# A threshold search by two bits a round on VectorE and ScalarE, and the small first loads moved to GpSimd

## The chip, the cores and the metric

The kernel runs on one core of one Trainium2 chip. The metric is the device time of one execution in microseconds (us). The engines are TensorE (PE in the profile's rows; PEld is its weight load), VectorE (DVE), ScalarE (ACT), GpSimd (POOL) and SyncE (SP). A letter q behind an engine's name means the queue that issues its transfers.

## What is computed

A GRU runs over 256 steps for 16 rows of width 512. Its 4096 states are the tokens of an "expert choice" layer: each of 16 experts takes its 256 best tokens by router probability, and what the one shared expert matrix makes of a token is weighted by the sum of the probabilities of the experts that took it.

```python
def cell(h, x):
    gi = x @ W_ih + b_ih
    gh = h @ W_hh + b_hh
    r = sigmoid(i_r + h_r);  z = sigmoid(i_z + h_z)
    n = tanh(i_n + r * h_n)
    return (1.0 - z) * n + z * h

S = softmax(xf @ router_w + router_b)        # 4096 tokens, 16 experts
G, idx = top_k(S.T, 256)
out = xf[idx] @ expert_w + expert_b
y = zeros(4096, 512).at[idx].add(G[..., None] * out)
return x + y
```

The top 256 of an expert are found as a threshold: the largest float32 that at least 256 of its 4096 probabilities reach. Probabilities are positive, so the order of the floats is the order of their bit patterns read as whole numbers.

## The kernel before, in words

**Head.** Constants (an identity, and masks that say which partitions belong to one expert) are made by GpSimd and VectorE in lines 86 to 106, in a pool of scratch memory that is given back afterwards and in which later tiles, the weights `wih` among them, come to lie. Then SyncE and ScalarE issue the weight loads in an order written out by hand (lines 272 to 285): for each of three gates of `W_ih` two loads of 512 KB, one on each queue; x of the first eight steps (`xa0`, eight loads of 32 KB, line 236) behind the first pair; then the three gates of `W_hh`; then x of the next eight steps (`xa1`, in the same buffer as `xa0`), the expert and router weights and two biases. GpSimd issues four bias loads (line 266) and four loads of the initial state (line 268). `turn_x` (line 252) transposes `xa`; the x parts of the first two pairs of steps (line 396) follow, and the recurrence.

**Recurrence.** For each step TensorE adds the products with `whh` (line 409), ScalarE takes sigmoid and tanh (lines 465, 486, 487), VectorE does the rest (lines 482 to 505). In what room is left TensorE computes the expert's product for even groups of eight steps. Fifteen groups are done so; 17 are *late groups*: the odd ones and group 30.

**Late groups.** A late group's product takes eight parts (`late_part`, line 136), each of four matmuls that the trace shows as eight records. `expert_for(n)` puts n parts into TensorE's queue at the place where it is called, so that they fill TensorE beside other work. At a group's fifth part the bank of the next group but one is filled with the expert's bias by ScalarE (`pe<-eb`, line 156; for the first three also cleared by TensorE, line 112); after the eighth ScalarE evicts the sum (`ht<-pe`, line 173). Five banks go round. Once the gate is known, a group isn't evicted any more: line 670 reads its bank.

**Search.** After the softmax the probabilities lie transposed in `sT`, 512 columns on each of 128 partitions, eight partitions an expert. The search sets one bit a round, from bit 29 down, in 30 rounds: VectorE compares all 512 columns with the candidate and sums along the partition (line 599), a TensorE matmul with `same_h` adds the eight partitions of an expert (line 604), `expert_for(2 or 3)` follows, and two small VectorE operations make the next candidate (lines 607 and 610). The order on TensorE, ScalarE and VectorE is the program's from line 570 on (`manual_schedule`).

**Routing and output.** Lines 621 to 662 settle ties and make `gate`, 32 columns of weights. Line 670 then makes the 32 output groups one after another, the fifteen early groups first and the late ones in order, and SyncE stores each (line 673, 256 KB). Where a late group isn't done, its remaining parts stand in TensorE's queue there.

Of the kernel before, what the change touches and what calls it, by code (L numbers as in the profile page):

```python
# [18 lines left out]
def kernel(  # L19
# [61 lines left out]
    same_h = const.tile([P, P], F16, name="same_h")  # L81
    before_f = const.tile([P, P], F32, name="before_f")
# [4 lines left out]
    make_identity(nc, ident)  # L87
    nc.gpsimd.memset(ones_b, 1.0)
    with tc.tile_pool(name="masks", bufs=1) as mk:
        shift = GH.bit_length() - 1  # L90
        at = mk.tile([P, 3], I32, name="at")
# [3 lines left out]
        at_f = mk.tile([P, 3], F32, name="at_f")  # L95
        nc.vector.tensor_copy(at_f, at)
        to_i = mk.tile([P, 2, E, GH], I32, name="to_i")
        nc.gpsimd.iota(to_i[:, 0, :, :], pattern=[[1, E], [0, GH]], base=0, channel_multiplier=0)
        nc.gpsimd.iota(to_i[:, 1, :, :], pattern=[[0, E], [1, GH]], base=0, channel_multiplier=0)
        to = mk.tile([P, 2, P], F32, name="to")  # L100
        nc.vector.tensor_copy(to, to_i.rearrange("p o e h -> p o (e h)"))
        nc.vector.tensor_scalar(same_f, to[:, 0, :], at_f[:, 1:2], None, ALU.is_equal)
        nc.vector.tensor_copy(same_h, same_f)
        nc.vector.tensor_scalar(before_f, to[:, 1, :], at_f[:, 2:3], None, ALU.is_gt)
# [79 lines left out]
    with (  # L184
# [23 lines left out]
        nc.gpsimd.memset(c0, 0.0)  # L208
# [51 lines left out]
        for dst, src in (  # L260
            (b_raw[0:1], b_ih.rearrange("(o g d) -> o g d", o=1, d=D)),
            (b_raw[1:2], b_hh.rearrange("(o g d) -> o g d", o=1, d=D)),
            (b_n, b_hh[2 * D :].rearrange("(o d) -> o d", o=1)),
            (b_r, router_b.rearrange("(o e) -> o e", o=1)),
        ):
            nc.gpsimd.dma_start(out=dst, in_=src)
        for j in range(KC):
            nc.gpsimd.dma_start(
                out=c0[QD * j : QD * j + B, :].rearrange("b (c i) -> b c i", c=KC), in_=columns(cond, j)
            )  # L270
        xa1 = new_xa()
        with tc.manual_schedule(engines={ET.SP, ET.Activation}):
            for i, gate in enumerate((0, 2, 1)):
                load_rows(wih[:, :, i, :], w_ih[:, gate * D : (gate + 1) * D], "(p c) n -> p c n")
                if i == 0:
                    for j in range(KC):
                        load_xa(0, xa0, j, queues)
            for gate in (0, 2, 1):
                load_rows(whh[:, :, gate, :], w_hh[:, gate * D : (gate + 1) * D], "(c p) n -> p c n")
            for j in range(KC):  # L280
# [138 lines left out]
        turn_x(0, xa0)  # L419
        xa_next = xa1  # L420
# [142 lines left out]
    with (  # L563
# [12 lines left out]

        ps = ps_s.tile([P, QG, P], F32, name="ps", tag="s")
# [13 lines left out]
        HIGH = 29  # L591
        cand = wk.tile([P, 1], I32, name="cand")
# [114 lines left out]
```

## Time and profile before

| what | us |
|---|---|
| median of 3 executions (lowest, highest) | 1201.27 (1201.14, 1209.14) |
| profiled execution: its time, its span | 1205.67, 1203.9 |
| TensorE, VectorE, ScalarE, GpSimd busy | 1163.5, 699.1, 323.3, 96.0 |
| first matmul with x (line 396); first matmul of step 1 (line 409) | 15.29; 29.11 |
| first compare of the search; `eq` behind it (line 621) | 1119.82; 1165.67 |
| first output row (line 670); first store issued (line 673) | 1172.89; 1173.67 |

Everything further goes by the profiled execution. Its rows have the start in us from the span's start, the duration in us, the engine, the line of the kernel, the operation, the tile written and the tiles read, the shapes, and behind x how many instructions the row merges; in brackets stands how long the engine was idle before and what ended it. The tables of windows give each engine's busy time in a stretch, with the instructions in brackets, then the clock granted to TensorE as a share of the full one, the share of time that the transfer engines were busy, and GB/s.

### The profile page before, as it was taken

How to read it: one execution, taken by the hardware profiler on the slowest of the kernel's cores; microseconds unless marked ns; L12 is line 12 of the kernel's file. 1: busy time of each engine (PE TensorE's matmuls, PEld its weight loads, DVE VectorE, ACT ScalarE, POOL GpSimd, SP SyncE). 2: the span in 40 equal slices, each digit the busy share in tenths (PEclk: the TensorE clock that was granted, in tenths of full speed). 3: DMA queues.
4: the chain of work that ended last, by engine and by line, in shares of the span. 5: the costliest groups of instructions: out<-in, count | busy, mean ns of one | idle time of the engine just before them, and what ended most of it. 6: DMA issues, size and time to landing. Idle time of an engine off the chain costs nothing. (4 is left out here: it accounts for less than half of the span.)

```text
span 1203.9 us, 80849 instructions
## 1 busy us (share of the span) xinstructions
PE 1163.5 (97%) x36490; PEld 1052.9 (87%) x36490; DVE 699.1 (58%) x3919; ACT 323.3 (27%) x1435; POOL 96.0 (8%) x398
## 2 busy tenths in 40 slices
PE   5999999999999999999999999999999999999897
PEld 3899999999999999989999999999999999998443
DVE  2555655565555655555565555565565556565776
ACT  0222222222222222322222222222222222222220
POOL 2000000000000000000000000000000000000000
PEclk9999999999999999999999999999999999999998
DMA  7200000000000000000000000000000000000008
GB/s 233 63 22 20 20 19 21 19 20 19 20 22 20 19 18 22 20 20 17 22 19 20 19 21 20 20 19 20 22 18 21 18 22 20 20 9 13 2 2 281
DMA packets 48730, 38.06 MB, mean 32 GB/s; under 512 B 7744, under 2 KB 40576, under 8 KB 48384
## 3 DMA queue, kind: packets, MB, share of 16 engines
q1 hardware_dynamic: 46176, 29.56, 8.4%
q8 instruction: 286, 4.69, 1.6%
q10 hardware_dynamic: 1952, 3.28, 0.8%
q14 instruction: 60, 0.49, 0.1%
q0 software_dynamic: 256, 0.05, 0.0%
HBM read 24.47 MB, written 8.39 MB: 27 GB/s over the span
## 5 line engine op out<-in xcount | busy, mean ns | idle before, releaser
L409 PE MATMUL ra<-whh,hs 128*16 128x128 f32 (+1 forms) x8192 | 348.4, 274 | 6.9 <-DVE zT L494 4.9
L409 PE MATMUL hn<-whh,hs 128*16 128x128 f32 (+1 forms) x8192 | 348.1, 273 | 0.8 <-DMA whh<-in_L_cond_W_hh_dram 0.8
L482 DVE TENSOR_TENSOR t<-r,hn 128x64 f32<-128x64 f32 x512 | 90.2, 217 | 369.8 <-PE hn L409 366.8
L396 PE MATMUL ra<-wih,xt 128*32 128x256 f32 x4096 | 288.4, 381 | 5.1 <-DMA wih<-in_L_cond_W_ih_dram 3.2
L409 PE MATMUL zz<-whh,hs 128*16 128x128 f32 (+1 forms) x8192 | 288.2, 273 | 3.0 <-DMA whh<-in_L_cond_W_hh_dram 1.9
L409 PEld LDWEIGHTS hn<-whh,hs 128*16 128x16 f32 (+1 forms) x8192 | 259.7, 104 | 1.2 <-DMA whh<-in_L_cond_W_hh_dram 1.1
L409 PEld LDWEIGHTS ra<-whh,hs 128*16 128x16 f32 (+1 forms) x8192 | 246.3, 103 | 15.5 <-issue 5.9
L409 PEld LDWEIGHTS zz<-whh,hs 128*16 128x16 f32 (+1 forms) x8192 | 240.5, 103 | 6.4 <-issue 3.5
L465 ACT ACTIVATE r<-ra 128x128 f32<-128x128 f32 x256 | 71.1, 278 | 591.3 <-PE ra L409 591.3
L396 PEld LDWEIGHTS ra<-wih,xt 128*32 128x32 f32 x4096 | 158.9, 110 | 38.3 <-issue 11.6
L486 ACT ACTIVATE n<-t 128x64 f32<-128x64 f32 x512 | 103.5, 248 | 192.8 <-DVE t L484 192.6
L396 PE MATMUL zz<-wih,xt 128*32 128x128 f32 x4096 | 146.6, 273 | 1.9 <-issue 1.4
L396 PEld LDWEIGHTS zz<-wih,xt 128*32 128x32 f32 x4096 | 129.0, 110 | 17.1 <-issue 5.0
L491 DVE STREAM_TRANSPOSE nT<-n 128x64 f32<-128x64 f32 x512 | 100.6, 234 | 57.3 <-ACT n L486 57.0
L494 DVE STREAM_TRANSPOSE zT<-zs 128x64 f32<-128x64 f32 x512 | 121.8, 238 | 3.6 <-ACT zs L487 3.0
L505 DVE TENSOR_TENSOR hs<-v,nT 128x32 f32<-128x32 f32 x512 | 101.9, 199 | 21.7
L502 DVE TENSOR_TENSOR v<-u,zT 128x32 f32<-128x32 f32 x512 | 104.4, 204 | 8.9
L363 PE MATMUL pe<-ewr,ht 128*32 128x136 f32 (+1 forms) x1920 | 108.2, 276 | 0.0
L484 DVE TENSOR_TENSOR t<-t,ra 128x64 f32<-128x64 f32 x512 | 88.2, 213 | 0.1
L363 PEld LDWEIGHTS pe<-ewr,ht 128*32 128x32 f32 x1920 | 76.5, 110 | 10.9 <-issue 0.5
L497 DVE TENSOR_TENSOR u<-hs,nT 128x32 f32<-128x32 f32 x512 | 78.3, 153 | 0.0
L136 PE MATMUL pe<-ewr,ht 128*32 128x256 f32 x1088 | 69.5, 395 | 1.9 <-ACT pe L156 1.9
(107 smaller groups left out, 513.6 us busy)
## 6 DMA issues: line engine op xcount, KB each, us to landing
xs<-in_x_dram SPq DMA_DIRECT2D x128, 64.0 KB, 2.3
out_dram<-xs SPq DMA_DIRECT2D x32, 256.0 KB, 3.9
xa<-in_x_dram SPq DMA_DIRECT2D x252, 32.0 KB, 2.2
wih<-in_L_cond_W_ih_dram SPq DMA_DIRECT2D x3, 512.0 KB, 5.5
wih<-in_L_cond_W_ih_dram ACTq DMA_DIRECT2D x3, 512.0 KB, 6.2
whh<-in_L_cond_W_hh_dram SPq DMA_DIRECT2D x3, 512.0 KB, 11.6
whh<-in_L_cond_W_hh_dram ACTq DMA_DIRECT2D x3, 512.0 KB, 11.2
ewr<-in_L_ffn_expert_w_dram SPq DMA_DIRECT2D x1, 1024.0 KB, 5.3
```

What stands on the lines that cost most here:

```text
L363: nc.tensor.matmul(pe[quadrant(j), at : at + w], ht[:, g, k, quadrant(j)], ewr[:, k, src : src + w], start=(k == 0), stop=(k == KC - 1), t ...
L396: nc.tensor.matmul(dst, lhs, rhs, start=False, stop=(k == KC - 1), tile_position=(0, QD * j), skip_group_check=True)
L409: nc.tensor.matmul(dst[quadrant(j, m)], lhs, columns(whh[:, k, gate_, :], j), start=False, stop=(k == KC - 1), tile_position=(0, QD * j), ...
L465: nc.scalar.activation(r, ra[p % 2][:, 0, :], AF.Sigmoid)
L482: nc.vector.tensor_tensor(t[half], r[:, cols], hn[p % 2][:, cols], ALU.mult)
L484: nc.vector.tensor_tensor(t[half], t[half], ra[p % 2][:, 1, cols], ALU.add)
L486: nc.scalar.activation(n[half], t[half], AF.Tanh)
L491: nc.vector.transpose(nT[half], n[half])
L494: nc.vector.transpose(zT[half], zs[:, halves[half][1]])
L497: nc.vector.tensor_tensor(u[half], hs[:, halves[half][2], slot(s), :], of_step(nT[half], odd), ALU.subtract)
L502: nc.vector.tensor_tensor(v[half], u[half], of_step(zT[half], odd), ALU.mult)
L505: nc.vector.tensor_tensor(hs[:, halves[half][2], slot(s + 1), :], v[half], of_step(nT[half], odd), ALU.add)
```

## The change

Three things change.

1. The search goes by two bits a round, 15 rounds. Bit patterns have 30 bits, more than a float32 holds as a whole number, so they are cut into the upper 16 (`high`, rounds 0 to 7) and the lower 14 (`both`: 0 to 2^14 on those that tie in the upper part, rounds 8 to 14), as float32 whole numbers. In each round three candidates are counted: VectorE compares all columns with the first and 192 columns with the second; ScalarE takes the sign of (candidate - key), with a sum, of all columns for the third and of the other 320 for the second. Two matmuls, the second with `less_half` (-0.5 times `same`), add both into one count, off by constants that `enough` and `short` make good. How many candidates pass, `k`, gives the two bits.
2. `expert_for(4)` stands in each round, instead of 2 and 3 in turn.
3. In the head, x of the first eight steps is loaded by GpSimd, behind the four bias loads and ahead of the initial state, and the order of GpSimd is the program's; the masks are made after `turn_x(0)`, in a part of `xs` that isn't loaded yet, and their scratch pool is gone.

In the compiled program the last four of the eight x loads on GpSimd wait for its first four loads to have landed, and the loads of the initial state wait for the first four of x.

```diff
-    make_identity(nc, ident)
-    nc.gpsimd.memset(ones_b, 1.0)
-    with tc.tile_pool(name="masks", bufs=1) as mk:
+
+    def make_masks():
+        make_identity(nc, ident)
+        nc.gpsimd.memset(ones_b, 1.0)
...
-        at = mk.tile([P, 3], I32, name="at")
+        at = xs[:, NG - 7, 0:3].bitcast(I32)
...
+        nc.vector.tensor_scalar(less_half, same_f, -0.5, None, ALU.mult)
...
-        with tc.manual_schedule(engines={ET.SP, ET.Activation}):
+        with tc.manual_schedule(engines={ET.SP, ET.Activation, ET.Pool}):
             for i, gate in enumerate((0, 2, 1)):
                 load_rows(wih[:, :, i, :], w_ih[:, gate * D : (gate + 1) * D], "(p c) n -> p c n")
-                if i == 0:
-                    for j in range(KC):
-                        load_xa(0, xa0, j, queues)
             for gate in (0, 2, 1):
                 load_rows(whh[:, :, gate, :], w_hh[:, gate * D : (gate + 1) * D], "(c p) n -> p c n")
+            for dst, src in (
...
+            ):
+                nc.gpsimd.dma_start(out=dst, in_=src)
+            for j in range(KC):
+                load_xa(0, xa0, j, (nc.gpsimd, nc.gpsimd))
+            nc.gpsimd.memset(c0, 0.0)
+            for j in range(KC):
+                nc.gpsimd.dma_start(
+                    out=c0[QD * j : QD * j + B, :].rearrange("b (c i) -> b c i", c=KC), in_=columns(cond, j)
+                )
...
         turn_x(0, xa0)
+        make_masks()
...
-        HIGH = 29
...
-        for bit in range(HIGH, -1, -1):
-            cnt = wk.tile([P, 1], F16, name="cnt")
-                nc.vector.tensor_scalar(
-                    ge, sT, cand.bitcast(F32), None, ALU.is_ge, ALU.add, accum_out=cnt
-                )
-            n = counts[:, bit : bit + 1]
-            nc.tensor.matmul(n, same_h, cnt, start=True, stop=True)
-            expert_for(2 + bit % 2)
-            nc.vector.tensor_scalar(off, n, float(TOPK), float(1 << bit), ALU.is_lt, ALU.mult)
...
-                nc.vector.scalar_tensor_tensor(
-                    nxt, cand, 1 << (bit - 1), off, ALU.bitwise_or, ALU.bitwise_xor
-                )
+        nc.vector.tensor_single_scalar(low, bits, -(1 << LOW), ALU.bitwise_and)
+        nc.vector.tensor_copy(high, low)
+        rounds = [1 << b for b in range(28, -1, -2)]
...
+        nc.vector.tensor_scalar(thr, steps, float(rounds[0]), below, ALU.mult, ALU.add)
+        keys = high
+        for r, q in enumerate(rounds):
+            last = r + 1 == len(rounds) or unit(r + 1) != unit(r)
+                nc.vector.tensor_scalar(
+                    ge, keys, thr[:, 0:1], None, ALU.is_ge, ALU.add, accum_out=cnt[r % 2][:, 0:1]
+                )
+                nc.vector.tensor_scalar(
+                    ge[:, 0:NV], keys[:, 0:NV], thr[:, 1:2], None, ALU.is_ge, ALU.add, accum_out=cnt[r % 2][:, 1:2]
+                )
+                nc.scalar.activation(
+                    sg, keys, AF.Sign, bias=thr[:, 2:3], scale=-1.0, accum_out=sgn[r % 2][:, 2:3]
+                )
+                nc.scalar.activation(
+                    sg[:, NV:], keys[:, NV:], AF.Sign, bias=thr[:, 1:2], scale=-1.0, accum_out=sgn[r % 2][:, 1:2]
+                )
+            if r == 0:
+                nc.vector.tensor_single_scalar(low, bits, (1 << LOW) - 1, ALU.bitwise_and)
+            n = counts[:, r, :]
+            nc.tensor.matmul(n, same_h, cnt[r % 2], start=True, stop=False)
+            nc.tensor.matmul(n, less_half, sgn[r % 2], start=False, stop=True)
+            expert_for(4)
+            if not last:
+                nc.vector.tensor_scalar(ahead, steps, float(rounds[r + 1]), below, ALU.mult, ALU.add)
+            nc.vector.scalar_tensor_tensor(passed, n, 0.0, enough, ALU.add, ALU.is_ge, accum_out=k)
+            if not last:
+                nc.vector.scalar_tensor_tensor(
+                    thr, k.to_broadcast([P, 3]), float(q), ahead, ALU.mult, ALU.add
+                )
+                nc.vector.scalar_tensor_tensor(nxt, k, float(q), below, ALU.mult, ALU.add)
+                continue
+            nc.vector.tensor_scalar(below, below, 0.5 * unit(r), None, ALU.add)
+            nc.vector.scalar_tensor_tensor(at, k, float(q), below, ALU.mult, ALU.add)
+            if r + 1 < len(rounds):
+                nc.vector.scalar_tensor_tensor(both, high, at, low, ALU.subtract, ALU.add)
+                keys = both
...
+        for i, at in enumerate(found.values()):
+            nc.vector.tensor_copy(found_i[:, i : i + 1], at)
+        nc.vector.tensor_tensor(found_i[:, 2:3], found_i[:, 0:1], found_i[:, 1:2], ALU.bitwise_or)
```

In the routing, `too_few` reads 45 counts plus `short` instead of 30 counts. `NV` is 192, `enough` and `short` are written by GpSimd ahead of the search.

## The prediction, made before the result was known

> **What bounds the kernel now.** The page's first table says TensorE 97% busy, but that is the mean over the recurrence. The change touches two other places, the first 30 us and everything after 1119.8 us, so I read those in order of time. First the timeline of the search, two rounds:
>
> ```profile
> 1151.77 0.16 PE L604 MATMUL counts<-cnt,same_h 128*128 128x1 f16 x1 [0.23 <-DVE ge L599]
> 1151.87 1.50 PE L136 MATMUL pe<-ewr,ht 128*32 128x256 f32 x24
> 1151.97 0.16 DVE L607 TENSOR_SCALAR off<-counts 128x1 int32<-128x1 f32 x1 [0.25 <-PE counts L604]
> 1152.16 0.16 DVE L610 SCALAR_TENSOR_TENSOR cand<-cand,off 128x1 int32<-128x1 int32 x1
> 1152.36 0.75 DVE L599 TENSOR_SCALAR_CACHE_REDUCE ge<-sT,cand 128x512 bf16<-128x512 f32 x1
> 1153.03 0.09 DVE L599 DVE_READ_ACCUMULATOR ge<-sT,cand 128x1 f16 x1
> 1153.08 0.59 ACT L173 COPY ht<-pe 128x512 f32<-128x512 f32 x1 [3.69 <-PE pe L136]
> 1153.30 0.18 PE L604 MATMUL counts<-cnt,same_h 128*128 128x1 f16 x1
> 1153.41 1.07 PE L136 MATMUL pe<-ewr,ht 128*32 128x256 f32 x16
> ```
>
> A bit is a loop count (PE), off, cand, compare (DVE), count: 1.53 us with three expert parts (x24) and 1.41 with two, 2.94 a pair. ScalarE's eviction L173 waits for TensorE, and nothing of the search waits for ScalarE. From the first compare (1119.82) to eq (1165.67) the search takes 45.85, of which 1.6 is a half clock early on: counts 1120.63 and 1123.68 stand 3.05 apart where 1.46 is usual.
>
> Second, TensorE's windows, cut at the steps of the granted clock, which all lie multiples of 3.41 us apart (columns: window, length, busy, count, granted clock, DMA share, GB/s):
>
> ```profile
> 25.27:28.68 3.41, 1.07 (x32) 1.00 0.20 52
> 28.68:32.09 3.41, 2.95 (x56) 0.51 0.80 259
> ...
> 1114.15:1117.56 3.41, 1.61 (x59) 1.00 0.03 5
> ...
> 1189.25:1192.66 3.41, 1.47 (x31) 1.00 1.01 336
> 1192.66:1196.07 3.41, 3.41 (x39) 0.50 0.96 323
> ```
>
> After a window with 1.07 or 1.47 us busy the next runs at half clock; after 1.61 it does not.
>
> Third, the head: the SyncE queue's waits, windows, and TensorE's rows.
>
> ```profile
> SPq L228 <- DVE row_of L106: 2.7, 1, 2.7
> 8.00:10.00 2.00, 0.51 (x16) 0.49 (x20) 0.00 (x0) 0.00 (x0) 0.00 (x0) 1.00 0.57 144
> 14.00:16.00 2.00, 0.71 (x8) 0.45 (x12) 0.00 (x0) 0.00 (x0) 0.14 (x1) 1.00 1.05 401
> 15.29 5.21 PE L396 MATMUL ra<-wih,xt 128*32 128x256 f32 x64 [3.23 <-DMA wih<-in_L_cond_W_ih_dram]
> 26.85 1.07 PE L409 MATMUL zz<-whh,hs 128*16 128x128 f32 x32 [1.86 <-DMA whh<-in_L_cond_W_hh_dram]
> ```
>
> The weights set the head: their loads begin only at 3.42, behind the masks, the transfers run half empty from 8 to 12, and step 0 waits for whh.
>
> Fourth, the tail:
>
> ```profile
> 1172.89 17.32 DVE L670 SCALAR_TENSOR_TENSOR xs<-ht,gate,xs 128x512 f32<-128x512 f32 x26
> 1173.67 25.97 SPq L673 DMA_DIRECT2D out_dram<-xs  x32
> 1190.90 0.59 ACT L156 COPY pe<-eb 128x512 f32<-128x512 f32 x1 [17.77 <-DVE xs L670]
> 1191.54 5.35 PE L136 MATMUL pe<-ewr,ht 128*32 128x256 f32 x64 [1.95 <-ACT pe L156]
> 1197.01 0.75 DVE L670 SCALAR_TENSOR_TENSOR xs<-pe,gate,xs 128x512 f32<-128x512 f32 x1 [3.51 <-issue]
> ```
>
> Stores run without a gap until about 1202, and the last expert group, which needs a bank freed by the 27th output row, ends just in time (1197.76).
>
> **The search, part by part.** Removed: 30 rounds. Added: 15, each with two compares on VectorE, two Sign activations on ScalarE, two count matmuls and four expert parts. Zero is the start of the second count matmul, which needs both engines.
> VectorE: passed at 0.20 (1151.77 to 1151.97), then its accumulator read, then thr at 0.55 (op spacing 0.19, read 0.09, rounded up); a Sign can start at 0.80.
> Signs: an exp takes 0.62 for 496 columns (L548) and 0.23 for 16, so 0.64 for 512 and 0.48 for 320. That ScalarE writes a sum is nowhere in this trace: nothing is the lower bound, 0.3 (a shortest ScalarE instruction, 0.23, and its spacing) the upper, each time; I take 0.15, nearer VectorE's read of 0.09. The second Sign waits for the first in the compiled program (0.05). Chain with the hand-over to TensorE (0.1): **1.57**, bounds 1.15 (with the 0.11 by which two copies overlap) and 1.95. VectorE's own two compares (0.75 and about 0.42 with reads) are done at about 2.15 and hide beside it.
> Odd rounds: 0.80 + 1.57 = 2.37. TensorE's four parts (0.43 each: x24 less x16) end at 2.0 and hide.
> Even rounds: here the compiled order on ScalarE is Sign, Sign, pe<-eb, **ht<-pe**, next Sign. The ht copy waits for the round's fourth part: 0.10 + 4 x 0.43 + 0.35 (at 1147.53 a batch started and its copy 0.78 later, one part and 0.35) = 2.16; the next ScalarE instruction follows 0.48 later, so the Sign starts at 2.64 although thr was ready at 0.80, and the next count is at **4.21**. Queued behind the copy are both Signs, for them TensorE's second count, and behind that the next expert parts.
> A pair, four bits, is 6.58; before, four bits were two pairs of 2.94, 5.88. Seven pairs 46.1; L112 in rounds 0, 2, 4 adds 0.25 each. The start (low, high at 0.49 each as eq, thr, hand-overs) puts the first Sign at 1121.07 and the first count at 1122.64; the change of keys between rounds 7 and 8 adds two small ops, a 0.74 pass and a thr, 1.2. Last count 1122.64 + 46.1 + 0.75 + 1.2 = 1170.7; eq 1.4 later (k, at, two casts, or) 1172.1, against 1165.67: **+6.4**; with the chain's bounds +0.5 and +11.7.
>
> **Clock.** In an even round TensorE idles from about 2.0 to 4.2. A 3.41 window around that holds under 1.4 busy, less than the 1.47 that was followed by half clock. About 1.3 of a pair's 6.58 are such window starts and windows come every 3.41: 0.38 a pair, 2.7 in seven; I take 3, at the 1.6 of the row above less some slack in odd rounds, 1.5: **+4.5**, bounds 0 and 10 (every pair, and the start).
> The Trainium skill, "TensorE: Matmul & The Clock Gate" (Why this matters for your kernels), asks for no idle gap above about 3 us; by it gaps of 2.2 would cost nothing and this term would be 0. The trace disagrees: 1189.25 to 1192.66 had gaps of only about 2 and was followed by 0.50.
> The skill's "ScalarE: Activation LUTs" (What ACT_TABLE_LOAD costs) gives an ACTIVATE with a per-partition bias 280 ns + 0.833 ns a column; estimated from it the two Signs are 1.25 instead of 1.12, about 2 us more over the search. The exp row, 0.62, looks like the page's immediate form.
>
> **Head.** Without the mask pool the weights can issue at 0.8, not 3.42, and without x's loads between them (4.97 on SyncE) the half-empty 8 to 12 goes: 2.6 + 1.6 earlier, so whh is whole at about 22.6, not 26.85. x moves to GpSimd: sixteen issues of about 0.5, of which the last four of x wait for the bias loads to land (the small one took 5.7 beside weights): last issue about 9.2, landing 2.2 to 5.8 later. I take L396's start at 15.0, was 15.29; bounds 12.5 and 16.5. From it h-parts at 21.7, r at 23.6, and step 1 2.73 later (1108.09 to 1110.82): 26.4, was 29.11. Step 1's half clock (r 2.93 after its first matmul; usually 1.66) may go too, 1.3. Together -4.0 at most likely inputs; I take **-3.5**, bounds -6.5 and 0. The masks and the cond load, now behind x on GpSimd, and ten mask ops on VectorE end by about 21, before step 0's first t: hidden, unless cond lands after 20.
>
> **Tail.** Expert parts done by the gate are 74, were 89, so 62 are left. Eight output rows come from banks, and group 14 needs group 9's row, the 25th: gate + 16.7 + copy 0.7 = 17.4. Then three groups of 3.42 end at gate + 27.7, last row 28.5, store and end about 4.5: gate + 33.0, was 31.0: **+2.0**, bounds 1 and 4 (a half clock). Eq to gate is unchanged; n_first's two further parts have 2 us of slack.
>
> **Sum.** 6.4 + 4.5 - 3.5 + 2.0 = +9.4 on the profiled execution (span 1203.9 to 1213.3, time 1205.67 to 1215.1). The median shown, 1201.27, is 4.4 below that execution; the difference carries over: **1210.7**.
>
> **Rivals.** (1) Forecast, Signs behind ht copies with some clock drops: 1205 to 1213, 0.45.
> (2) Not slower: sums on ScalarE come free (chain 1.15) and idle gaps stay too short for the clock. +0.5 + 0 - 4.5 + 2 gives 1199; it decides below a chain of about 1.3. For it: the page shows ScalarE 27% busy; against it: the accumulator has to be read somewhere. 1192 to 1205, 0.18.
> (3) Clock: nearly every even round is followed by half clock, when odd rounds become TensorE's (four parts 3.4). +6.4 + 10 - 3 + 2.5 gives 1217; it decides when the idle part passes 2 us. 1213 to 1225, 0.29.
> (4) The change does what it says: ScalarE truly beside VectorE, all rounds 2.37. 14 x 2.37 + 1.2 + 1122.64 puts eq at 1158.4, -7.2; with -3.5 and +2, 1192.5; 0.05. Against it the compiled order.
> (5) x through GpSimd late by 5 or more, so the head is lost as well: about 1217, 0.03.
> Measurement and drift make 1% (12 us) the bound for "no change". Faster by over 1% needs (4) with a better head: 0.05; slower by over 1% is (3), (5) and the top of (1): 0.36; the rest 0.59. Range 1198 to 1222 leaves 0.2 out.
>
> **What would show it.** Even rounds near 4.2 and odd near 2.4, with Sign's idle time put down to nothing but the ht copy before it; windows at 0.50 between 1120 and 1172; wih issued before 1.5; step 1 near 26; the last bank's copy near gate + 18. Wrong if ScalarE's sums cost nothing or over 0.3, if half-clock windows are absent or in every pair, or if x lands after 17.

## The result, and the profile after

The changed kernel takes 1214.96 us (median of 6 runs, 1212.68 to 1218.67) where the kernel before takes 1204.14 on the same chip (1201.14 to 1209.48): a ratio of **1.0086, 95% interval 1.0063 to 1.0109**. It is slower, by about 10 us, and within the 1% that was called no change. The forecast was 1210.7, that is 9.4 over a base of 1201.27.

The profiled execution of the changed kernel has a time of 1212.68 and a span of 1210.9, against 1205.67 and 1203.9 before. That is 7.0 more, not 10. Cut into stages, the two profiles stand like this (us):

| stage | before | after | difference |
|---|---|---|---|
| start to step 2's r (head) | 36.23 | 36.15 | -0.1 |
| step 2's r to the last state (recurrence) | 1079.35 | 1076.89 | -2.5 |
| last state to sT complete (softmax, transposes) | 4.08 | 4.12 | 0.0 |
| sT complete to eq (search) | 46.01 | 53.82 | +7.8 |
| eq to the gate | 7.22 | 7.27 | +0.1 |
| gate to the end (tail) | 31.01 | 32.65 | +1.6 |

Here r is the first sigmoid of a step on ScalarE, the last state is taken where its copy into `ht` starts, sT are the transposed probabilities, eq is the first comparison behind the search, and the gate is taken at the start of the first output row, 0.04 us after `gate` is written.

The recurrence runs the same code in both kernels; over this study's profiles the stretch was between 1074.7 and 1080.6 us with no relation to the edits. Its -2.5 is a difference between executions and not a gain. Without it the profiles differ by +9.5, which agrees with the timed medians (7.6 to 13.1 by the interval).

**The search.** The timeline of ScalarE in the changed kernel, from the end of one round's Signs to the end of the next round's, with the copies of an even round between them (columns: start, duration, engine, line, operation, output and input, shape, count, and in brackets the idle time before it and what ended it):

```profile
1156.37 0.56 ACT L647 ACTIVATE sg<-both,thr 128x320 bf16<-128x320 f32 x1
1156.84 0.19 ACT L647 ACTIVATION_READ_ACCUMULATOR sg<-both,thr 128x1 f16 x1
1156.93 0.58 ACT L160 COPY pe<-eb 128x512 f32<-128x512 f32 x1
1159.18 0.58 ACT L177 COPY ht<-pe 128x512 f32<-128x512 f32 x1 [1.67 <-PE pe L140]
1159.66 0.72 ACT L644 ACTIVATE sg<-both,thr 128x512 bf16<-128x512 f32 x1
1160.28 0.19 ACT L644 ACTIVATION_READ_ACCUMULATOR sg<-both,thr 128x1 f16 x1
1160.51 0.56 ACT L647 ACTIVATE sg<-both,thr 128x320 bf16<-128x320 f32 x1
1160.98 0.19 ACT L647 ACTIVATION_READ_ACCUMULATOR sg<-both,thr 128x1 f16 x1
```

and TensorE, with VectorE's thresholds, beside it:

```profile
1157.08 0.16 PE L655 MATMUL counts<-sgn,less_half 128*128 128x3 f16 x1
1157.18 1.93 PE L140 MATMUL pe<-ewr,ht 128*32 128x256 f32 x32
1157.56 0.16 DVE L665 SCALAR_TENSOR_TENSOR thr<-k,ahead 128x3 f32<-128x3 f32 x1
1159.04 0.18 PE L654 MATMUL counts<-cnt,same_h 128*128 128x3 f16 x1
1161.22 0.16 PE L655 MATMUL counts<-sgn,less_half 128*128 128x3 f16 x1 [2.00 <-ACT sg L647]
```

The copy ht<-pe (L177) waits 1.67 us for the round's fourth expert part. The Sign behind it starts at 1159.66, although VectorE had written the thresholds by 1157.72 (L665, 1157.56 plus 0.16). So the counts (L655) of this round and the next stand 4.14 us apart, and 2.29 after the round before, where ScalarE has nothing to wait for. TensorE idles for 2.00 us.

TensorE's windows of 3.413 us, cut at the steps of the granted clock (columns: window, length, busy time and count of PE, PEld, DVE, ACT, POOL, then granted clock, DMA share, GB/s):

```profile
1116.20:1119.62 3.42, 0.63 (x4) 0.43 (x3) 2.52 (x9) 1.47 (x4) 0.00 (x0) 1.00 0.00 0
1119.62:1123.03 3.41, 3.06 (x30) 1.54 (x34) 2.42 (x13) 1.07 (x3) 0.00 (x0) 0.50 0.00 0
1123.03:1126.44 3.41, 1.40 (x26) 0.60 (x18) 0.24 (x3) 1.95 (x5) 0.00 (x0) 1.00 0.00 0
1126.44:1129.86 3.42, 3.42 (x38) 1.53 (x34) 1.78 (x11) 1.47 (x4) 0.00 (x0) 0.50 0.03 5
...
1143.51:1146.93 3.42, 1.43 (x26) 0.63 (x18) 1.09 (x4) 1.95 (x5) 0.00 (x0) 1.00 0.01 2
1146.93:1150.34 3.41, 3.41 (x33) 1.36 (x32) 2.64 (x12) 1.21 (x3) 0.00 (x0) 0.50 0.01 2
```

Three windows of the search run at half clock, each after one with 0.63, 1.40 or 1.43 us of work. The intervals between the counts show the price: 5.73, 3.33, 4.61, 2.29, 4.35, 2.29, 4.13, then 3.78 at the change of keys, and from there 4.13 and 2.29 in turn. Rounds 2 and 4, which start fresh banks, cost 4.35 at the full clock (round 4 here, both in e8 and e9), and round 0, which starts one too, is taken at the same; so the clock cost 1.38 + 1.04 + 0.26 = 2.7 us here; the third half-clock window fell beside the change of keys, where TensorE isn't waited for, and cost nothing.

**The head.** GpSimd's issues of x, and the two instructions that the first step waits for, by time:

```profile
3.40 2.06 POOL L239 DMA_DIRECT2D xa<-in_x_dram  x4
7.22 0.51 POOL L239 DMA_DIRECT2D xa<-in_x_dram  x1 [1.77 <-DMA xs<-in_L_cond_b_ih_dram]
8.92 1.52 POOL L239 DMA_DIRECT2D xa<-in_x_dram  x3 [1.18 <-DMA xs<-in_L_cond_b_hh_dram]
17.38 1.08 DVE L255 STREAM_TRANSPOSE xt<-xa 128x512 f32<-128x512 f32 x1 [4.40 <-DMA xs<-in_cond_dram]
18.51 6.32 PE L400 MATMUL ra<-wih,xt 128*32 128x256 f32 x64 [5.88 <-DVE xt L255]
```

The weights do issue early (from 0.74), but x's eight loads go out between 3.40 and 10.44, the last four behind two waits, and x is transposed only at 17.38, where it was 11.81 before. The last of x had landed at 17.10; the row names the initial state, whose first load landed at 17.40, when the transposition had begun. The first input product starts at 18.51 instead of 15.29. Step 0's r comes at 27.96 (24.62 before), step 1's at 32.14 (32.04), since W_hh is there by then and no half-clock window falls on step 1, as one did before.

**The tail.** VectorE's rows, ScalarE's bank copies and TensorE's parts after the gate:

```profile
1178.25 16.00 DVE L744 SCALAR_TENSOR_TENSOR xs<-ht,gate,xs 128x512 f32<-128x512 f32 x24
1194.95 1.91 ACT L160 COPY pe<-eb 128x512 f32<-128x512 f32 x3 [16.67 <-DVE xs L744]
1195.59 10.57 PE L140 MATMUL pe<-ewr,ht 128*32 128x256 f32 x192 [1.06 <-ACT pe L160]
1206.28 0.75 DVE L744 SCALAR_TENSOR_TENSOR xs<-pe,gate,xs 128x512 f32<-128x512 f32 x1 [2.70 <-DMA out_dram<-xs]
```

The bank copy stands at gate + 16.70; 24 matmul parts (x192) follow it in 10.57, against 8 (x64) in 5.35 before (partly at half clock), and the last row starts at gate + 28.03.

### The profile page after: what moved, and what is told of

The parts are those of the page before. It is cut to its first block, busy times and chain, and to the rows that moved or that the text cites. A ratio compares the mean times of both kernels' runs of the same rounds, so it can differ in the third digit from the quotient of the medians.

```text
span 1210.9 us, 80961 instructions
## 1 busy us (share of the span) xinstructions
PE 1159.3 (96%) x36490; PEld 1050.0 (87%) x36490; DVE 694.9 (57%) x3943; ACT 342.7 (28%) x1493; POOL 100.1 (8%) x419
## 4 chain that ended last, share of the span: by engine, by line
PE 88%; DVE 6%; ACT 2%; issue 1%; DMA 1%; POOL 0%; SPq 0%; DVEq 0%; ACTq 0%; POOLq 0%
PE ra L413 19%; PE hn L413 18%; PE ra L400 17%; PE zz L413 17%; PE zz L400 9%; PE pe L367 5%; PE pe L140 3%; DVE xs L744 1%; ACT sg L644 1%; DVE nT L496 1%; DVE t L487 1%; ACT sg L647 1%; DVE zT L499 1%; ACT n L491 1%; DMA xs<-in_L_cond_b_hh_dram 1%
## 5 line engine op out<-in xcount | busy, mean ns | idle before, releaser
L413 PE MATMUL ra<-whh,hs 128*16 128x128 f32 (+1 forms) x8192 | 344.2, 273 | 8.1 <-DVE zT L499 6.5
L413 PE MATMUL hn<-whh,hs 128*16 128x128 f32 (+1 forms) x8192 | 344.0, 273 | 0.0
L400 PE MATMUL ra<-wih,xt 128*32 128x256 f32 x4096 | 286.6, 382 | 7.3 <-DVE xt L255 5.9
L413 PEld LDWEIGHTS ra<-whh,hs 128*16 128x16 f32 (+1 forms) x8192 | 242.3, 103 | 17.5 <-issue 7.1
L413 PEld LDWEIGHTS hn<-whh,hs 128*16 128x16 f32 (+1 forms) x8192 | 255.7, 103 | 0.3
L400 PEld LDWEIGHTS ra<-wih,xt 128*32 128x32 f32 x4096 | 156.4, 111 | 41.3 <-issue 7.4
L400 PE MATMUL zz<-wih,xt 128*32 128x128 f32 x4096 | 145.4, 273 | 0.7 <-issue 0.4
L400 PEld LDWEIGHTS zz<-wih,xt 128*32 128x32 f32 x4096 | 127.9, 110 | 16.1 <-issue 3.0
```

Of the source, the lines that this page charges most:

```text
L400: nc.tensor.matmul(dst, lhs, rhs, start=False, stop=(k == KC - 1), tile_position=(0, QD * j), skip_group_check=True)
L413: nc.tensor.matmul(dst[quadrant(j, m)], lhs, columns(whh[:, k, gate_, :], j), start=False, stop=(k == KC - 1), tile_position=(0, QD * j), ...
```

## Experiments

The kernels of e1 to e4, of e5 to e7 and of e8 to e11 each ran together on one chip, and share their runs of the kernel before; the times of different groups are compared by their ratios.

### e1: the eviction after the round's Signs

The copy ht<-pe is held back and issued on ScalarE after the next round's two Signs; in the routing, where no Signs follow, it goes between the expert parts. All else is the changed kernel.

```diff
-                        nc.scalar.copy(wide(g), pe)
+                        held.append((g, pe))
...
+    held = []
+
+    def evict():
+        while held:
+            g, pe = held.pop(0)
+            nc.scalar.copy(wide(g), pe)
...
                 nc.scalar.activation(
                     sg[:, NV:], keys[:, NV:], AF.Sign, bias=thr[:, 1:2], scale=-1.0, accum_out=sgn[r % 2][:, 1:2]
                 )
+            evict()
...
+        evict()
         expert_for(4)
+        evict()
...
         expert_for(6)
+        evict()
```

> The changed kernel, but each eviction ht<-pe stands on ScalarE behind the next round's two Signs instead of ahead of them. Theory (ScalarE's order sets the even rounds): every round becomes what odd rounds are, 2.29 us between counts, the search from sT to eq falls from 53.8 to about 40, no window at half clock after the first, gate to end stays near 32.7; the time is 13 to 15 us below the changed kernel, some 3 below the one before (ratio 0.996 to 0.999). Rival (TensorE's four parts, or the Signs themselves, set even rounds): even rounds stay at 4.1 and the ratio to before at 1.009. Second rival (what the search gives is lost again in the tail): search 40, but gate to end over 40, ratio above 1.003.

Measured: 1201.54 (12 runs) against 1202.87, ratio 0.9992 (0.9976 to 1.0007). The search is 40.73 us, 13.1 below the changed kernel and 5.3 below the kernel before; the tail is unchanged at 32.63. By the ratios e1 is 0.94%, some 11 us, below the changed kernel, a little less than the 13 to 15 expected. ScalarE's timeline in e1, first after round 2, then in later rounds:

```profile
1127.94 0.59 ACT L160 COPY pe<-eb 128x512 f32<-128x512 f32 x1 [1.04 <-PE pe L116]
1128.47 0.72 ACT L651 ACTIVATE sg<-high,thr 128x512 bf16<-128x512 f32 x1
...
1145.91 0.57 ACT L186 COPY ht<-pe 128x512 f32<-128x512 f32 x1
1146.79 0.72 ACT L651 ACTIVATE sg<-both,thr 128x512 bf16<-128x512 f32 x1 [0.32 <-DVE below L677]
1148.20 0.58 ACT L160 COPY pe<-eb 128x512 f32<-128x512 f32 x1
1149.10 0.72 ACT L651 ACTIVATE sg<-both,thr 128x512 bf16<-128x512 f32 x1 [0.32 <-DVE below L677]
```

In the warm rounds that start no fresh bank ScalarE now waits 0.31 to 0.32 us for VectorE ahead of the first Sign, the copies lie in the gap, and these rounds are 2.29 to 2.31 whether even or odd. After rounds 0, 2 and 4 the order is still not right: the bank fill pe<-eb waits for TensorE's clearing matmuls (L116; 1.04 us after round 2) and stands ahead of the next Sign as the eviction did, so that rounds 2 and 4 take 3.07. No run moved it. The two Signs and their reads cost the same as in the changed kernel. So the order on ScalarE, and neither its sums nor TensorE's four parts, made the even rounds long. With shorter rounds TensorE idles little, and after one half-clock window at its start the search has no other; of the 13.1 us some 2 are the clock's.

### e2 and e3: the head alone

e2 is the changed kernel with the old head (masks first, x on SyncE and ScalarE between the W_ih loads, small loads unordered on GpSimd); e3 is the kernel before with the new head. The core of e2, against the changed kernel (e3 is the same turned round, on the kernel before):

```diff
-        with tc.manual_schedule(engines={ET.SP, ET.Activation, ET.Pool}):
+        with tc.manual_schedule(engines={ET.SP, ET.Activation}):
             for i, gate in enumerate((0, 2, 1)):
                 load_rows(wih[:, :, i, :], w_ih[:, gate * D : (gate + 1) * D], "(p c) n -> p c n")
+                if i == 0:
+                    for j in range(KC):
+                        load_xa(0, xa0, j, queues)
...
-            for j in range(KC):
-                load_xa(0, xa0, j, (nc.gpsimd, nc.gpsimd))
```

> The new search with the head of before (masks first in their own pool, x on SyncE and ScalarE behind the first pair of weights, initial state unordered). If the new head is worth the forecast 3.5 us, this is 3.5 slower than the changed kernel: ratio to before 1.0115 to 1.012. If it is worth nothing, as step 2 starting at 34.58 instead of 34.66 suggests, the ratio stays at 1.0086 within 0.001.

> The kernel before with the new head alone. Forecast's worth: ratio 0.997. Worth nothing: 1.000 within 0.001, x's transposition ending near 18.5 us and step 1 starting near 30.5, step 2 near 34.6.

Measured: e2 1216.43 (5 runs), ratio 1.0103 (1.0086 to 1.0120), against 1.0086 for the changed kernel; e3 1203.16 (12 runs), ratio 0.9992 (0.9980 to 1.0005). The new head is worth some 2 us by e2, with an uncertainty of some 3, which decides for neither expectation, and about 1 by e3, whose interval (2.4 us gained to 0.6 lost) holds no change and excludes the 3.5 of the forecast. In e3's profile x is transposed at 17.03 and step 0's r stands at 26.97, nearly as late as in the changed kernel, so the late x belongs to the head and not to the search.

One profile of each head is too little to compare them. With the old head step 2's r stood at 36.23 before and at 37.79 in e4, both with a half-clock window on step 1, but at 34.05 in e2, where none fell there. With the new head it stood between 34.76 and 36.30 in five profiles (the changed kernel, e1, e3, e9, e10), none with such a window.

### e4: the old search with two parts in every round

The kernel before, with two expert parts in each of the 30 rounds instead of two and three in turn. The tail then gets what the rounds leave.

```diff
-            expert_for(2 + bit % 2)
+            expert_for(2)
```

> The kernel before with two expert parts in every round of its search instead of three and two in turn, so that 60 instead of 75 are done by the end of it and 62 instead of 47 are left at the gate, as in the changed kernel. Theory (what is left of the expert parts, and the bank that group 14 waits for, set the tail): rounds of 1.41, the search 1.8 shorter, gate to end 33 instead of 31; together 0.998 to 1.001. Rival (the stores alone set the tail): gate to end stays at 31, ratio 0.9985.

Measured: 1202.09 (12 runs), ratio 0.9994 (0.9982 to 1.0007). Gate to end is 32.93, as the theory had it (31.01 before, and 30.13 in e3, whose tail is the same code): the tail grows with the parts that the search leaves over. The search shrank by 3.9 where 1.8 was expected. About 1.6 of the other 2 us is the clock: e4's half-clock window stood at 1115.54 to 1118.95, before the first compare, so its rounds never ran cold, while the kernel before had its window at 1120.98 to 1124.39, inside the search.

### e5, e6, e7: x first, and the order of the rows

e6 is the changed kernel with x's first eight loads moved back to SyncE and ScalarE, ahead of the weights. e5 is the same edit on e1. e7 is e5 with the late groups' rows spread between the ready ones.

The head's edit, in e5 and e6:

```diff
+            for j in range(KC):
+                load_xa(0, xa0, j, queues)
             for i, gate in enumerate((0, 2, 1)):
                 load_rows(wih[:, :, i, :], w_ih[:, gate * D : (gate + 1) * D], "(p c) n -> p c n")
...
-            for j in range(KC):
-                load_xa(0, xa0, j, (nc.gpsimd, nc.gpsimd))
```

The rows' order, in e7:

```diff
-        for g in [g for g in range(NG) if g not in late_groups] + late_groups:
+        ready = [g for g in range(NG) if g not in late_groups] + late_done
+        rest = [g for g in late_groups if g not in late_done]
+        rows = []
+        for n in (4, 4, 4, 5, 4, 3):
+            rows += ready[:n] + rest[:1]
+            ready, rest = ready[n:], rest[1:]
+        for g in rows + ready + rest:
```

> The late eviction of e1_late_evict, and a head of a third kind: the small loads stay on GpSimd and the masks stay late, as in the changed kernel, but the first step's x goes first on SyncE's and ScalarE's queues, ahead of the W_ih loads, and not over GpSimd. Theory (x's eight loads over GpSimd's queue, each landing 5.8 to 7.2 us after its issue and some waiting for b_ih and b_hh, put the transpose of x at 17.4 and ate the head's gain): x lands near 4, xt is transposed near 6, the weights start some 3 us later than in the changed kernel, the first x-part starts between 10.4 and 12.5 and step 0's r ends between 19.5 and 22 (27.96 in the changed kernel, 24.62 before); step 1's r ends near 25 to 28 (32.14, 32.04). The total is 4 to 7 us below e1_late_evict's 1201.5, a ratio to the kernel before of 0.993 to 0.996. Rival (the head is bound by the transfers of the weights whoever issues them, and step 1 waits for W_hh): step 0's r comes early but step 2's r stays at 35 to 36, and the total is within 2 us of e1_late_evict, 0.998 to 1.001.

> The changed kernel with the x-first head of e5 alone; search and tail as in the changed kernel. Theory (x over GpSimd's queue ate the head's gain): 4 to 7 us below the changed kernel, a ratio to the kernel before of 1.003 to 1.005, with the search at 53.8 from sT to eq and the tail at 32.7. Rival (bound by the weights' transfers): within 2 us of the changed kernel, 1.007 to 1.009, with step 2's r at 35 to 36 as there.

> e5 with the output's rows in another order: the six groups that are finished late stand between the ready ones (after 4, 4, 4, 5, 4 and 3 of them) where the changed kernel has 24 ready rows first. Theory (the tail grew from 31.0 to 32.6 since ScalarE's next copies and with them TensorE's last parts wait 16 us behind 24 rows on VectorE, and the last rows then come one matmul group of 2.7 us apart): from the gate to the end 31 to 31.5 and 1.2 to 1.6 us less than e5. Rival (the tail is set by the stores and by VectorE's row time alone, not by the order): the tail stays at 32.4 to 32.9 and the total is within 0.6 us of e5.

Measured: e5 1196.82 (9 runs) against 1200.92, ratio **0.9961 (0.9944 to 0.9978)**; e6 1212.71 (6 runs), ratio 1.0097 (1.0078 to 1.0116); e7 1196.84 (7 runs), ratio 0.9958 (0.9941 to 0.9976).

The head did about as expected in all three; in e5 step 1's r, at 28.23, came a little late, with a half-clock window on step 1. From the timeline of e5:

```profile
4.70 1.08 DVE L262 STREAM_TRANSPOSE xt<-xa 128x512 f32<-128x512 f32 x1 [3.80 <-DMA xa<-in_x_dram]
11.18 5.90 PE L407 MATMUL ra<-wih,xt 128*32 128x256 f32 x64 [0.15 <-DMA wih<-in_L_cond_W_ih_dram]
20.50 0.63 PE L420 MATMUL hn<-whh,hs 128*16 128x128 f32 x16 [1.24 <-DMA whh<-in_L_cond_W_hh_dram]
23.34 1.07 PE L420 MATMUL zz<-whh,hs 128*16 128x128 f32 x32 [1.33 <-DMA whh<-in_L_cond_W_hh_dram]
```

x is transposed at 4.70 instead of 17.16, the first product starts at 11.18, and what is late next is W_hh, twice (1.24 and 1.33 us). Step 0's r is at 21.64 (26.56 in e1) and step 2's at 32.88 (34.76). By the ratios e5 gains 0.31% on e1, 3.7 us, with an uncertainty of some 2.8. So x's late landing ate the head's gain; the rival, weights that land late anyway, takes back a part of it only.

e5 changed two things for x, its queue and its place ahead of the weights, and no run changes one alone, but the traces point to the second. On SyncE's and ScalarE's queues ahead of the weights the eight loads landed 1.8 to 2.3 us after issue in e5. On the same queues beside the weights, in the kernel before, the first six took 5.7 to 6.0, hardly less than GpSimd's 5.8 to 7.2 in the changed kernel, and the last two, issued when the first pair of weights had landed or nearly so, 3.0 and 2.5. So a load is late beside the weights on any of the three queues; what GpSimd's order adds is the two waits for the biases to land.

e6 missed: its head was 4.9 us earlier at step 2's r (31.25), and its total is no better than the changed kernel's. Its search took 56.86 us, 3.0 more, and its recurrence 2.2 more, both with the same code. The windows of e6:

```profile
1112.71:1116.12 3.41, 1.06 (x10) 0.64 (x4) 2.47 (x10) 0.70 (x2) 0.00 (x0) 1.00 0.00 0
1116.12:1119.54 3.42, 2.26 (x22) 1.18 (x26) 3.21 (x15) 1.67 (x5) 0.00 (x0) 0.50 0.00 0
1119.54:1122.95 3.41, 2.23 (x21) 0.70 (x13) 0.00 (x0) 1.42 (x4) 0.00 (x0) 0.50 0.00 0
1122.95:1126.36 3.41, 2.61 (x25) 1.29 (x29) 1.68 (x9) 2.19 (x7) 0.00 (x0) 0.50 0.00 0
1126.36:1129.78 3.42, 3.42 (x38) 1.36 (x34) 1.69 (x9) 0.59 (x1) 0.00 (x0) 0.50 0.02 5
1129.78:1133.19 3.41, 1.41 (x26) 0.61 (x22) 0.08 (x1) 1.95 (x5) 0.00 (x0) 1.00 0.00 0
1133.19:1136.60 3.41, 3.41 (x37) 1.45 (x29) 1.60 (x9) 1.47 (x4) 0.00 (x0) 0.50 0.00 0
```

Four half-clock windows in a row and a fifth, against three in the changed kernel. sT was complete 1.65 us before the first of them (at 1114.47), and 2.46 us before it in the changed kernel (at 1117.16). In e6 the count intervals were 6.29, 3.74, 5.41 and 3.59 before they became the usual 4.35 and 2.29. Against those warm intervals (4.35 and 2.29 in turn) the clock cost 5.8 us there.

e7's tail is 31.7 in its profile against 32.9 in e5's, a little outside the 31 to 31.5 that was expected. VectorE and TensorE after the gate, in e7:

```profile
1158.58 26.97 PE L140 MATMUL pe<-ewr,ht 128*32 128x256 f32 x496
1182.22 0.75 DVE L761 SCALAR_TENSOR_TENSOR xs<-pe,gate,xs 128x512 f32<-128x512 f32 x1 [2.34 <-PE pe L140]
1185.67 0.75 DVE L761 SCALAR_TENSOR_TENSOR xs<-pe,gate,xs 128x512 f32<-128x512 f32 x1 [2.70 <-PE pe L140]
```

TensorE now runs its 62 remaining parts (x496) without a gap, and the last rows wait for it alone. That the tail is only 1.2 shorter says that the parts themselves, and not the row order, make most of it. The medians of e5 and e7 are the same, so this gain is seen in one profile and not in the timing.

### e8 to e11: the clock, and x first again

e9 is the changed kernel, and e8 is e6, with work on TensorE that does nothing but keep it busy: two expert parts repeated in each even round, written to a PSUM tile that is never read. e10 is the changed kernel and e11 is e6, once more on the same chip.

```diff
+        idle = ps_s.tile([P, QG, P], F32, name="idle", tag="s").rearrange("p q n -> p (q n)")
+        def fill(n):
+            for part in range(n):
+                k, h = divmod(part, 2)
+                cols = slice(HD * h, HD * (h + 1))
+                for j in range(KC):
+                    q = slice(QD * j, QD * (j + 1))
+                    nc.tensor.matmul(
+                        idle[q, 0:HD],
+                        ht[:, 0, k, q],
+                        ewr[:, k, E:][:, cols],
+                        start=True,
+                        stop=True,
+                        tile_position=(0, QD * j),
+                        skip_group_check=True,
+                    )
...
             expert_for(4)
+            if r % 2 == 0:
+                fill(2)
```

> The kernel of e6_x_first with idle work on TensorE: after the four parts of every even round it repeats two more parts into a PSUM tile that nothing reads (8 of its 16 x 256-column fp32 products each, 0.97 us in all at the full clock). The even rounds leave TensorE idle for some 2 us, so the products lie beside ScalarE's eviction and Signs. Theory (the search is lengthened by half-clock windows, which follow a window of 3.41 us with less than some 1.45 to 1.57 us of full-speed TensorE work; e6_x_first had five of them, 3.1 us more search than the changed kernel): at most the first window or two are at half clock, warm even rounds stay at 4.13, sT to eq is 51.5 to 53.5 (56.86 in e6_x_first), and the total is 2 to 4.5 us below e6_x_first. Rival (the rounds are long for another reason, ScalarE or VectorE, and the clock only goes along): sT to eq stays at 55 to 58 or the filled rounds get longer by the 0.97 us, and the total is not below e6_x_first.

> The changed kernel with the same two repeated parts in every even round. Theory (half-clock windows): sT to eq 51.5 to 53.5 instead of 53.82, one half-clock window at the search's start and perhaps a second, none later; the total 1 to 4 us below the changed kernel, 1.005 to 1.008. Rival (ScalarE or VectorE make the rounds long): not below the changed kernel, 1.008 to 1.011, or above it if the products stand in the path.

> The changed kernel itself, on the same chip as e6_x_first's repetition and the two filled kernels. Whether the head with x first gains in the changed kernel is open: its profile had step 2's r 4.9 us earlier than the changed kernel's, but its search 3.1 us longer and its recurrence over 1 us longer, and e5_x_first_late_evict gained 3.7 us over e1_late_evict. Expected here 1.008 to 1.010, with a search between 52.5 and 57 by the windows that it meets.

> e6_x_first again. Theory (the head's gain of 4 to 5 us is real and the two profiles differed by the clock windows that the search met, which stand differently in each execution): on the median of the same chip 2 to 5 us below e10_changed_again, 1.004 to 1.007. Rival (the search of this kernel always meets more half-clock windows, since the windows stand in a fixed place from the program's start): within 1.5 us of e10_changed_again, with three or more half-clock windows at the search's start again.

Measured, all against 1201.92:

| kernel | median us | ratio (95%) | search | half-clock windows in it |
|---|---|---|---|---|
| e10, changed | 1213.51 | 1.0103 (1.0081 to 1.0125) | 53.74 | 3 |
| e11, x first | 1209.22 | 1.0063 (1.0041 to 1.0085) | 55.43 | 3 |
| e9, changed, filled | 1212.20 | 1.0087 (1.0067 to 1.0107) | 53.09 | 2 |
| e8, x first, filled | 1210.65 | 1.0079 (1.0058 to 1.0100) | 53.09 | 2 |

The windows of e9:

```profile
1119.54:1122.95 3.41, 2.83 (x26) 1.35 (x30) 2.63 (x15) 1.27 (x4) 0.00 (x0) 0.50 0.00 0
1122.95:1126.36 3.41, 3.37 (x33) 1.26 (x25) 0.00 (x0) 1.77 (x5) 0.00 (x0) 0.50 0.00 0
1126.36:1129.78 3.42, 3.02 (x51) 1.65 (x55) 2.25 (x14) 1.66 (x6) 0.00 (x0) 1.00 0.02 5
1129.78:1133.19 3.41, 2.35 (x45) 1.18 (x38) 1.12 (x5) 2.53 (x6) 0.00 (x0) 1.00 0.00 0
```

With the filling no window of the search after the first two holds less than 1.84 us of work, no half clock follows, and both filled kernels have the same search to the hundredth, 53.09, with intervals of 4.35 and 2.29 right after the first round (6.29). That settles that the long early rounds of the unfilled kernels are the clock's. The even rounds stay at 4.13: the 0.97 us of filling lies wholly beside ScalarE. The expected gain in time didn't come: e9 is 1.3 below e10 and e8 1.4 above e11, all within the intervals. Two things worked against it. The first round is 6.29, against 5.66 and 6.05 in e10 and e11 (by the filling, or by the place of the window: it was 6.29 in e6 and e2 too, without filling); and the last round's filling stands before the parts that precede n_first, so that eq to the gate is 8.10 instead of 7.27. For e9 that leaves nothing of the 0.65 that its search gained. e8's search gained 2.3 on e11's, and why the time shows none of it stays open.

x first is better than the changed kernel by 0.40% in e11 against e10 (the intervals overlap by a hair), by 0.08% in e8 against e9, and worse by 0.11% in e6 against the first measurement of the changed kernel. The cut at step 2's r flatters x first: in e6, e8 and e11 step 3's r follows 0.5 to 1.0 us later than usual, behind a pause of TensorE that the profile explains by no wait. At step 3's r x first is ahead by 3.9 us (e6 against the changed kernel), 3.4 (e11 against e10) and 4.6 (e8 against e9). In the profiles sT was complete at 1114.47, 1112.15 and 1113.98 with x first, and at 1117.16, 1115.36 and 1117.32 without: on average 3.1 us earlier, with executions' drift of some 2 us in each. In the two unfilled pairs the search gave back 3.0 and 1.7 of it. The rival that the windows stand in a fixed place from the program's start is refuted: their edges, taken modulo 3.413 us, were at 0.05, 1.52, 3.37, 2.66, 2.79 and 3.38 in six profiles. What the x-first head is worth in time beside the changed search stays open, between about -1 and 5 us by the three pairs; beside the late eviction it is 3.7, give or take 2.8.

## Why the prediction was right

The total was right: +9.4 forecast on the profile, +9.5 found between the stages without the recurrence, a ratio of 1.0078 forecast and 1.0086 measured. (The median itself, 1214.96, lies above the 1205 to 1213 of rival 1, the forecast, since the three executions shown had a median 2.9 below that of the six.) The terms weren't right. Search and clock together were set at +10.9 and measured +7.8; the head at -3.5 and measured -0.1; the tail at +2.0 and measured +1.6. Two errors of about 3 us cancelled, which is luck: nothing ties the head to the search.

**Even rounds at 4.21 behind the ht copy, odd at 2.37: right.** 4.13 and 2.29 were measured, and e1 shows the mechanism by removing it. The pair was 0.15 too long, 1.05 us over seven pairs, because the thresholds are ready at 0.73 after a count, not 0.80, and the ht copy at 2.10, not 2.16.

**The ScalarE chain of 1.57: right,** 1.56 measured (1159.66 to 1161.22). Its parts were off in opposite directions: a Sign of 512 takes 0.72, not 0.64, a Sign of 320 0.56, not 0.48, and the sum's read is 0.19, not 0.15, but Sign, read, Sign and read overlap more than was allowed. The Trainium skill's "ScalarE: Activation LUTs" (What ACT_TABLE_LOAD costs) has 280 ns + 0.833 ns a column for a per-partition bias, which would be 0.71 and 0.55: the trace agrees with it here, within 0.02.

**Rival 2 (the sums come free, the gaps stay too short for the clock): wrong on both counts,** as the reads of 0.19 and the windows after 1.40 and 1.43 show. **Rival 4 (all rounds 2.37)** is what e1 makes true, at 2.30 in all warm rounds but those that start fresh banks, by the order on ScalarE alone: the order was the only thing against it, as the prediction said.

**The clock, +4.5: the mechanism right, the size too large.** 2.7 was measured in the changed kernel's profile, about 2.6 in e10's, 5.8 in e6's and 4.3 in e11's. The bounds of 0 and 10 hold. The estimate of three drops was met, at 1.38, 1.30 (1.04 and 0.26 in two rounds) and 0 where 1.5 each was taken: the third fell beside the change of keys, where VectorE and ScalarE set the pace. "Nearly every even round" (rival 3) didn't happen, since once warm a pair leaves at least 1.5 us of work in nearly every window. The rule of the Trainium skill's "TensorE: Matmul & The Clock Gate" (Why this matters for your kernels) that was weighed there, no idle gap above about 3 us, would have made this term 0. The first half-clock window did follow a gap of 3.08 us, but the other two followed windows whose longest gap was 2.01, so the trace decides against the rule as a sufficient condition. Nor was a window's work the whole of it: in the prediction's own profile the window behind the one of 1.61 held 1.77 us and was followed by half clock.

**The change of keys at 1.2 and the end at 1.4:** 1.49 and 1.05. They cancel nearly.

**The head, -3.5: wrong.** The step that failed is "I take L396's start at 15.0": the same instruction (L400 in the changed kernel) started at 18.51, beyond the upper bound of 16.5. The issues were nearly foreseen (last one about 9.2; it started at 9.92), but x's landing was set between 2.2 and 5.8 us after it, and the eight loads took a median of 6.5, the last 7.17. Three bias loads ahead of them, on which the issues wait, took 5.6 to 6.7 beside the weights, where they had taken 1.7 to 2.3 when they were issued ahead of the weights. "Wrong if x lands after 17" came about (transpose at 17.38). What kept the head from being a loss is the other half of the step, which was right: weights issued at 0.74, W_hh whole in time, and no half clock on step 1 (e2's profile shows that the old head can be without it too), so that the 3.3 us lost at step 0 were won back by step 1. This is rival 5's mechanism: the gain of the head was lost, all of it by these two profiles, all but about 1 us by e3's time, and no more than that.

**The tail, +2.0: right,** +1.6. Gate + 16.7 for the release was met (the copy starts at gate + 16.70). The last row was at gate + 28.03 instead of 28.5.

**What the difference of the two profiles could have misled to:** 7.0 against 10 timed. The recurrence, equal in code, was 2.5 us shorter in the changed kernel's profiled execution. Only stage by stage do the numbers close.

## What to carry to other kernels

When work is shared out to an engine that also serves another chain, read that engine's compiled order first: an eviction that waits for the last matmul of a round and stands ahead of the critical operation costs the whole wait, and moving it behind that operation took 13 us off the search in the profile and some 11 off the time (e1). Small loads that must land early should go out ahead of the bulk transfers, since beside them they took about three times longer here, on whichever queue, and what waits for them is issued later still. x first, then the weights, was the order that paid together with the late eviction (e5: 0.9961 of the kernel before). And a stage that leaves TensorE a little too idle pays in half-clock windows whose number depends on where they happen to fall, so that one profile of such a stage can differ from the next by 3 us.

## What the runs showed of the hardware

The granted clock went with the work done in the window before, and hardly with its longest idle gap. All thirteen profiles were cut into windows of 3.413 us along the clock's steps over the last softmax and the search, with busy time at half clock counted half. Every window with up to 1.41 us of work was followed by half clock. From 1.42 to 1.49 both occurred. From 1.53 on the full clock followed, with two exceptions, 1.73 in e3 and 1.77 in the profile before:

```profile
1117.57:1120.98 3.41, 1.77 (x24) 0.95 (x19) 2.43 (x10) 0.60 (x2) 0.00 (x0) 1.00 0.00 0
1120.98:1124.39 3.41, 3.41 (x37) 1.49 (x33) 1.35 (x7) 0.59 (x1) 0.00 (x0) 0.50 0.00 0
```

In both, 0.81 us of the work is the transposes of the probabilities. Whether transposes count less is not shown: a window of e11 with 1.62, part of it transposes, was followed by the full clock. e6 stayed cold for four windows since 2.26, 2.23 and 2.61 busy at half clock are 1.13, 1.12 and 1.31 of work. The grid of windows keeps its period exactly within an execution, and its place differs from one execution to the next.

A sum written by ScalarE ends in an instruction of its own of 0.19 us, on VectorE it is 0.09. And eight loads of 32 KB over GpSimd's queue landed a median of 6.5 us after issue while the weights were on their way, and six of them over the other two queues 5.7 to 6.0 (the kernel before); with x ahead of the weights on those two queues, issued from 0.74 on, they took 1.8 to 2.3, and x was transposed from 4.70 (e5).
